# A four-layer graph network on one core: layer 0 in nine blocks instead of eight, its layernorm split over three engines, and the dense part fused in place

## The chip, the cores and the metric

The kernel runs on one core of one Trainium2 chip, in one launch. The time is device time in microseconds, the median of three executions. Each profile is of one further execution. PE is TensorE, DVE is VectorE, ACT is ScalarE, POOL is GpSimd, SP is SyncE; PEld is TensorE's loading of weights. L12 means line 12 of the kernel.

## The reference

x is 4096 x 256 in float32, adj is 4096 x 4096 in int32 with ones at a density of 1/128. Four layers follow each other, each `x = x + layer(relu(layernorm(x)), adj)`:

```python
# layer 0: attention, and a dense part on top of it
Wh = h @ W                                      # 4096 x 256
e = Wh @ a_src + (Wh @ a_dst).T                 # one term per row, one per column
e = where(e > 0, e, 0.2 * e)
attn = softmax(where(adj > 0, e, -9e15), axis=1)
h_attn = attn @ Wh
h_enh = silu(ln(Wh @ fe1)) @ fe2                # biases left out in this listing
B, C, dt = split(Wh @ W_bcdt)
ab = (softmax(dt + A) * B) @ abp
hp, z = split((Wh * ab) @ W_hz)
hs = ((hp * silu(z) + hp * D) @ out_w) * (1 + C @ cp_w)
g = sigmoid(silu(ln(concat(h_attn, hs) @ g1)) @ g2)
out = ln(g * h_attn + (1 - g) * hs + h_enh)
# layer 1: mean over neighbours, then a matrix
# layer 2: attention as in layer 0 with slope 0.01, then elu
# layer 3: softmax(Q K^T masked by adj + identity) @ V
```

## The kernel before

x lives in SBUF as `xs`, 32 row tiles of 128 rows. Work is laid out in blocks of `BT` = `RB` = 4 row tiles. The program is written as Python loops; a scheduler then decides where each instruction stands in the queue of its engine, and every engine works through its queue in order. Tiles come from pools with a fixed number of buffers; a tile that takes over a buffer waits until the last use of the tile before it.

**Layer 0, preparation (`block0`, L416).** For each of eight blocks: three units of adj are fetched and turned (`fresh`, L348), four tiles of x are loaded, layer-normed (`preln`, L124: statistics on DVE, the power -1/2 on POOL, and one activation for each tile on ACT), transposed on PE (`transposed_block`, L138: PSUM is copied half by DVE, half by ACT), and multiplied by W (`project`, L201). W carries two more columns, W a_src and W a_dst, which `weights` (L178) computes with DVE, so the product gives Wh and both attention terms. DVE copies the two terms into `sd` (L208), ACT copies the rest into `v` (L209), which has a last column of ones.

**A unit of adj** is 128 rows x 1024 columns. POOL's queue loads it, turning int32 into bf16. PE transposes its eight 128x128 squares into PSUM (`cT`, one buffer), and ACT's exponential makes of 0 and 1 a very large and a very small number ("codes", L362), into `turned`. SP's queue also writes the codes to DRAM (`codesT`), for the later layers.

**Layer 0, attention (class `Attention`).** A block of four row tiles goes over 32 column tiles, two at a time: 16 pairs. `reach` (L216) runs 19 pairs ahead of it, and finds each row's largest logit: DVE takes a running minimum over codes minus the column's term (L229), ACT and PE turn the result, and small DVE instructions make two row terms, `ab`. These are written to DRAM and read back spread over all partitions (`ab_row`, L251 and L253). `logits` (L258) makes y with DVE (L265) and subtracts the codes with POOL (L269). `run` (L271) then lets ACT take the exponential (L295) and PE multiply y by v (L306), three pairs later, summing in four accumulators, the last column being the softmax denominator. A float32 product is two passes on PE. Between these steps `ahead` (L367) turns one more unit of a later block.

**Layer 0, dense part (`dense`, L561).** Eight blocks, each a long chain of products, layernorms, and gates over four row tiles. It is a generator with some thirty steps; a new block starts every sixteen steps, so that two are in work at a time. After each of the first sixteen steps `count` (L550) counts one unit of adj for layer 1 with two Sign activations on ACT (L556); `ask` (L544) loads the unit ahead of time through POOL's queue, into four buffers. Towards the end of a block, `f` (L682) receives the gate's product; its buffer is also that of `henh` (L645). `f` is then layer-normed, scaled and added to `xt` (x read again) by POOL (L695, L696), which writes `xs`.

**Layer 1 to 3** follow with their own preparations. Layer 2 uses the same class `Attention`.

## Time and profile before

| | us |
|---|---|
| median of three runs | 3072.19 (3071.23 to 3072.98) |
| profiled execution | 3071.94 |
| its span, first to last instruction | 3070.0 |
| first product of layer 0's attention | at 118.9 |
| its last | at 638.4 |
| end of layer 0's dense part | at about 1250 |
| layer 1 | 1250 to 1550 |
| preparation of layer 2 | 1550 to 1618 |
| layer 2's attention | 1618 to 2097 |
| layer 3 | 2097 to 3070 |

In lines that list busy times, the columns are the stretch, its length, then the busy time (and number of instructions) of PE, PEld, DVE, ACT and POOL, the granted clock of TensorE as a share of full speed, the mean busy share of the 16 DMA engines, and the GB/s that they moved. In the timeline a line gives start, duration, engine, line, operation, out<-in, shapes and count; in brackets stands the idle time of the engine before it and what ended it. In lists of waits, "A <- B: 44.3, 7, 7.0" means that A waited for B 44.3 us in total, seven times, at most 7.0 us. "q" after an engine's name is its queue of DMA issues.

### The profile page before, as it was taken

What the parts mean: (1) busy time and instruction counts of PE and PEld (TensorE: products, weight loads), DVE (VectorE), ACT (ScalarE), POOL (GpSimd) and SP (SyncE); (2) the same over time, 40 slices, a digit from 0 to 9 for tenths busy, and PEclk for the clock granted to TensorE, in tenths of its full rate; (3) what the DMA queues carried; (4) which work ended last, traced back from release to release, by engine and by line L of the source; (5) the groups of instructions that cost most, each with busy time, mean ns of one, the idle gap of its engine ahead of it and who ended that gap; (6) DMA issues with size and microseconds to landing.
All of it is one profiled execution on the core that took longest, in us unless ns stands there. A gap on an engine that the chain in (4) does not pass through costs nothing.

```text
span 3070.0 us, 34819 instructions
## 1 busy us (share of the span) xinstructions
PE 2868.8 (93%) x13344; PEld 2341.7 (76%) x13344; DVE 1847.3 (60%) x3298; ACT 1271.1 (41%) x1924; POOL 952.6 (31%) x727
## 2 busy tenths in 40 slices
PE   5799999999999999699968999999999999999999
PEld 4688888866565555588857888788888888888888
DVE  5766766424444444544479888845866666666653
ACT  5555665469999962400044434443211211211211
POOL 3556665534544443100016555561000000000000
PEclk9799999999999999799988999999999999999999
DMA  8566665244544420234222222102111111111100
GB/s 208 130 137 143 127 137 132 66 65 73 79 76 77 75 47 7 88 124 142 91 110 76 89 79 72 71 8 69 59 37 46 49 37 43 52 37 40 53 7 7
DMA packets 105366, 235.18 MB, mean 77 GB/s; under 512 B 10704, under 2 KB 26576, under 8 KB 97008
## 3 DMA queue, kind: packets, MB, share of 16 engines
q0 software_dynamic: 39328, 73.56, 15.6%
q1 hardware_dynamic: 64480, 158.68, 15.0%
q8 instruction: 104, 1.70, 0.2%
q10 hardware_dynamic: 1392, 0.72, 0.1%
q14 instruction: 62, 0.51, 0.1%
HBM read 262.22 MB, written 37.81 MB: 98 GB/s over the span
## 4 chain that ended last, share of the span: by engine, by line
PE 26%; issue 25%; DVE 4%; POOL 2%; DMA 1%; ACT 1%; POOLq 0%; DVEq 0%; ACTq 0%
PE acc L306 11%; PE acc L764 8%; PE s L150 3%; PE mm L150 2%; PE acc L1001 2%; DVE run L229 1%; POOL y L269 1%; DVE y L265 1%; DMA turned<-codesT 1%; POOL out_dram L1014 1%; POOL pl_rs L116 0%; DVE pl_st L121 0%; ACT y L295 0%; ACT h L133 0%; DVE hT L109 0%
## 5 line engine op out<-in xcount | busy, mean ns | idle before, releaser
L306 PE MATMUL acc<-v,y 128*128 128x257 f32 x4096 | 927.7, 385 | 46.1 <-ACT y L295 23.5
L306 PEld LDWEIGHTS acc<-v,y 128*128 128x128 f32 x4096 | 776.3, 192 | 160.5 <-ACT y L295 24.1
L269 POOL TENSOR_TENSOR y<-y,turned 128x1024 f32<-128x1024 f32 x256 | 547.1, 2150 | 313.9 <-DVE y L265 267.1
L295 ACT ACTIVATE y<-y,sdst 128x512 f32<-128x512 f32 x512 | 342.9, 714 | 368.1 <-POOL y L269 367.9
L265 DVE SCALAR_TENSOR_TENSOR y<-ab_row,cdst,b 128x512 f32<-128x512 f32 x512 | 361.7, 742 | 187.9 <-PE acc L306 116.6
L1001 PE MATMUL acc<-v,y 128*128 128x257 f32 x2048 | 454.5, 380 | 0.4 <-DVE rden L1009 0.4
L150 PE MATMUL s<-qT,hT 128*128 128x256 f32 x2048 | 445.2, 380 | 0.7 <-ACT qT L949 0.7
L150 PEld LDWEIGHTS s<-qT,hT 128*128 128x128 f32 x2048 | 389.9, 190 | 53.2 <-ACT qT L949 1.4
L1001 PEld LDWEIGHTS acc<-v,y 128*128 128x128 f32 x2048 | 387.9, 190 | 55.1 <-issue 0.8
L994 ACT ACTIVATE y<-y 128x1024 f32<-128x1024 f32 x128 | 132.2, 1055 | 714.3 <-DVE y L993 710.1
L229 DVE SCALAR_TENSOR_TENSOR run<-turned,sd,run 128x512 f32<-128x512 bf16 x496 | 373.0, 752 | 48.4 <-DMA turned<-codesT 26.8
L1014 POOL DMA_DIRECT2D out_dram<-o x32 | 17.4, 542 | 933.7 <-DVE rden L1009 930.5
L556 ACT ACTIVATE sign<-a,limits 128x1024 bf16<-128x1024 bf16 x256 | 293.9, 1148 | 16.1 <-DMA a<-in_adj_dram 10.4
L764 PE MATMUL acc<-v,eq 128*128 128x512 f32 x1024 | 239.3, 395 | 0.0
L963 DVE SCALAR_TENSOR_TENSOR y<-code,s 128x512 f32<-128x512 bf16 x256 | 175.7, 687 | 100.5 <-PE s L150 100.3
L764 PEld LDWEIGHTS acc<-v,eq 128*128 128x128 f32 x1024 | 192.9, 189 | 44.7 <-DVE eq L760 0.3
L993 DVE TENSOR_TENSOR y<-y,top 128x1024 f32<-128x1024 f32 x128 | 146.2, 1214 | 43.0 <-PE top L987 43.0
L970 DVE TENSOR_TENSOR mx<-mx,y 128x512 f32<-128x512 f32 x224 | 154.9, 691 | 7.4
L362 ACT ACTIVATE turned<-cT,log_wide 128x1024 bf16<-128x1024 bf16 x128 | 141.4, 1105 | 32.1 <-PE cT L357 31.9
L150 PE MATMUL mm<-kept 128*128 128x512 f32 x288 | 135.6, 605 | 9.4 <-ACT kept L508 7.3
L760 DVE TENSOR_SCALAR eq<-code 128x4096 fp32r<-128x4096 bf16 x32 | 73.4, 2292 | 114.9 <-PE acc L764 114.9
L357 PE MATMUL cT<-identb,adj_t 128*128 128x128 bf16 x1024 | 83.2, 226 | 38.1 <-ACT turned L362 19.5
(209 smaller groups left out, 2779.4 us busy)
## 6 DMA issues: line engine op xcount, KB each, us to landing
adj_t<-in_adj_dram POOLq DMA_DIRECT2D x128, 256.0 KB, 4.6
codesT<-turned SPq DMA_DIRECT2D x32, 1024.0 KB, 5.3
a<-in_adj_dram POOLq DMA_DIRECT2D x128, 256.0 KB, 4.2
code<-codesT SPq DMA_DIRECT2D x128, 256.0 KB, 3.8
turned<-codesT SPq DMA_DIRECT2D x32, 1024.0 KB, 4.8
code<-codesT SPq DMA_DIRECT2D x64, 512.0 KB, 4.9
ab_row<-l_ab_d SPq DMA_DIRECT2D x16, 512.0 KB, 4.7
xs<-in_x_dram SPq DMA_DIRECT2D x8, 512.0 KB, 8.3
```

Source lines behind the costliest of these rows:

```text
L150: nc.tensor.matmul(out=ps, lhsT=lhsT_of(k), rhs=rhs_of(k), start=(k == 0), stop=(k == n - 1))
L229: nc.vector.scalar_tensor_tensor(st["run"], code, self.sd[:, j, 1:2], st["run"], ALU.subtract, ALU.min)
L265: nc.vector.scalar_tensor_tensor(y[:, :, k, :], st["ab"][:, 0, :, :], self.cdst[:, c + k : c + k + 1], st["b"], ALU.add, ALU.max,)
L269: nc.gpsimd.tensor_tensor(y, y, mask[:, :, c % QT : c % QT + 2, :], ALU.subtract)
L295: nc.scalar.activation(y[:, :, k, :], y[:, :, k, :], AF.Exp, bias=self.sdst[:, c + k : c + k + 1],)
L306: nc.tensor.matmul(out=accs[b][r], lhsT=y[:, r, k, :], rhs=self.v[:, c + k, :], start=(c + k == 0), stop=(c + k == NT - 1),)
L556: nc.scalar.activation(sign, came[g], AF.Sign, bias=limits[:, v : v + 1], accum_out=over[:, t, v, q : q + 1],)
L764: nc.tensor.matmul(out=acc, lhsT=eq[:, ts(c, P)], rhs=v1[:, c, :, :], start=(c == 0), stop=(c == NT - 1),)
L963: nc.vector.scalar_tensor_tensor(y[:, :, c : c + 2, :], st["code"][:, :, c : c + 2, :], -BIG / UNIT, ps, ALU.mult, ALU.add,)
L970: nc.vector.tensor_tensor(mx, mx, y[:, :, c : c + 2, :], ALU.max)
L993: nc.vector.tensor_tensor(part, part, top, ALU.subtract)
L1001: nc.tensor.matmul(out=accs[r], lhsT=st["y"][:, r, c, :], rhs=v3[:, c, :], start=(c == 0), stop=(c == NT - 1),)
```

## The change

**Two half blocks.** The blocks of layer 0's attention are now nine: rows 0 and 1, rows 2 and 3, then seven of four. A block needs the codes of its own rows and the column terms of all rows, so the first needs 8 units of adj, not 16. The units come in the order of the blocks. The first 8 of them have buffers of their own in the preparation; one unit, not three, is turned for each block of x, and twelve before the attention's loop begins. codesT is written once both halves are there.

**Row terms of the first block.** They are spread over the partitions by PE, as four products with a 4 x 4 x 128 selection matrix `picks`, and copied by ACT and DVE; all other blocks go through DRAM as before.

**Layernorm.** The mean is taken off with a change of sign, by ACT (one tile of four), DVE (two) and POOL (one). The transposed copy in PSUM gets relu with scale -1 on ACT, both halves. The factor 1/sqrt(var) is applied after W, in ACT's copy of the product.

**v.** It has the ones in its first column, Wh in the next 256, and the two attention terms behind. One ACT copy of 258 columns takes the place of DVE's copy of two and ACT's of 256, in layers 0 and 2. `sd` is gone.

**Loads.** W and the a rows go through ACT's queue in layer 0, all eight loads of x are issued at the beginning, from SP and ACT in turn, and four units of adj ahead of all of POOL's other loads. W_bcdt and the rows with it are loaded by SP in the last block of the attention into free adj buffers, and the six small DVE instructions with them move there too. The cast of `identb` is on POOL.

**Dense part.** `f` is written into `xs` itself (the block's attention result, last read before), no longer into `henh`'s buffer. `count` asks for one unit less ahead, with the four buffers left.

```diff
-    nc.vector.tensor_copy(identb, ident)
+    nc.gpsimd.tensor_copy(identb, ident)
...
-            evac(k, hT[:, k, :], ps)
+            if turned:
+                nc.scalar.activation(hT[:, k, :], ps, AF.Relu, scale=-1.0)
+            else:
+                evac(k, hT[:, k, :], ps)
...
-                nc.vector.tensor_copy(sd[:, t, :], ps[:, D : D + 2])
-                nc.scalar.copy(self.v[:, t, 0:D], ps[:, 0:D])
+                row = self.v[:, b * BT + i, 1 : D + 3]
+                if rs is None:
+                    nc.scalar.copy(row, ps)
+                else:
+                    nc.scalar.mul(row, ps, rs[:, i : i + 1])
...
+            if self.picks is not None and b == 0:
+                ps = self.ps_top.tile([P, 2 * n, P], F32, tag="top", name="spread")
+                for k in range(2 * n):
+                    nc.tensor.matmul(
+                        out=ps[:, k, :], lhsT=self.picks[:, k, :], rhs=abT, start=True, stop=True
+                    )
+                for v in range(2):
+                    evac(1 - v, st["ab"][:, v, :, :], ps[:, ts(v, n), :])
+                return
             nc.sync.dma_start(out=self.ab_d[b].rearrange("v r i -> (v r) i"), in_=abT)
...
+            cuts = [(0, 2), (2, 2)] + [(t, RB) for t in range(RB, NT, RB)]
+            units = [
+                (at // RB, q, r % RB)
+                for at, n in cuts for q in range(NQ) for r in range(at, at + n)
+            ]
+            def needed(n):
+                b, c = n // PPB, n % PPB
+                if b >= len(cuts):
+                    return len(units)
+                return cuts[b][0] * NQ + cuts[b][1] * NQ * (c + 1) // PPB
...
             def ahead(n):
-                if n + UPB + FRESH < NRB * UPB:
-                    fresh(n + UPB + FRESH)
+                fresh(needed(n + PPB + FRESH))
...
+                load(4)
+                att.weights(
+                    wp, work, w["L0_gnn_W"], (w["L0_gnn_a_src"], w["L0_gnn_a_dst"]), nc.scalar
+                )
+                for b in range(NB):
+                    (nc.scalar if b % 2 else nc.sync).dma_start(
+                        out=xs[:, ts(b, BT), :],
+                        in_=x[ts(b, BW), :].rearrange("(t p) d -> p t d", p=P),
+                    )
                 def block0(b):
                     xb = xs[:, ts(b, BT), :]
-                    for g in range(3 * b, 3 * b + 3):
-                        fresh(g)
...
-                    preln(small, xb, xb)
+                    for i in range(BT):
+                        mean = mv[:, i, 0:1]
+                        if i == 0:
+                            nc.scalar.activation(
+                                xb[:, i, :], xb[:, i, :], AF.Identity, scale=-1.0, bias=mean
+                            )
+                        else:
+                            (nc.gpsimd if i == BT - 1 else nc.vector).tensor_scalar(
+                                xb[:, i, :], xb[:, i, :], mean, -1.0, ALU.subtract, ALU.mult
+                            )
+                    rs = rstd_of(small, mv, BT, "pl")
+                    load(2 * b + 6)
+                    fresh(b + 1)
                     yield
-                    hT = transposed_block(work, pst, xb, "hT")
+                    hT = transposed_block(work, pst, xb, "hT", turned=True)
                     yield
-                    att.project(b, hT, psm)
+                    att.project(b, hT, psm, rs)
                     yield
-                    for n in range(2 * b, 2 * b + 2 if b < NB - 1 else PPB + LEAD):
+                    for n in range(2 * b, 2 * b + 2):
                         att.reach(n)
                 run_staggered([block0(b) for b in range(NB)], 2)
...
+                fresh(needed(PPB + FRESH - 1))
+                for n in range(PPB, PPB + LEAD):
+                    att.reach(n)
...
             def count(g):
-                ask(g + AHEAD)
+                ask(g + AHEAD - 1)
...
-                f = d.tile([P, BT, D], F32, tag="henh", name="f")
+                f = ha
...
-                nc.gpsimd.tensor_tensor(ha, f, xt, ALU.add)
+                nc.gpsimd.tensor_tensor(f, f, xt, ALU.add)
...
-            ask(AHEAD - 1)
+            ask(AHEAD - 2)
```

## The prediction

> **What bounds the kernel now.** I began with the slices of the page, to see where TensorE is not full, then took busy times by stage.
>
> ```profile
> PE   5799999999999999699968999999999999999999
> ACT  5555665469999962400044434443211211211211
> PEclk9799999999999999799988999999999999999999
> ```
>
> ```profile
> 118.90:184.70 65.80, 64.09 (x349) 55.19 (x350) 49.18 (x82) 40.41 (x57) 49.72 (x32) 0.97 0.39 81
> 184.70:638.40 453.70, 438.44 (x2499) 377.62 (x2497) 281.45 (x457) 240.57 (x332) 271.15 (x190) 1.00 0.51 115
> 638.40:1250.00 611.60, 557.44 (x2049) 354.82 (x2047) 272.32 (x565) 484.28 (x767) 267.21 (x246) 0.97 0.40 63
> 1550.00:1618.30 68.30, 42.15 (x197) 33.13 (x197) 59.51 (x189) 35.09 (x78) 10.98 (x10) 0.82 0.24 100
> ```
>
> Columns: stretch, length, then PE, PEld, DVE, ACT, POOL busy, clock, DMA share, GB/s. The attention of layer 0 (its first block, then the other seven) is full of PE. The dense part is not: PE 557 of 612 us, ACT 484. The preparation of layer 2 leans on DVE (59.5 of 68.3). Layers 1 and 3 are not edited. The 118.9 us ahead of attention are the first thing to look at:
>
> ```profile
> 40.00:60.00 20.00, 17.29 (x132) 14.34 (x131) 12.67 (x35) 18.82 (x35) 6.39 (x10) 1.00 0.81 184
> 60.00:80.00 20.00, 18.33 (x147) 15.81 (x146) 13.01 (x34) 19.89 (x37) 4.91 (x10) 1.00 1.02 230
> 80.00:100.00 20.00, 14.18 (x118) 11.89 (x117) 16.22 (x36) 13.40 (x20) 4.84 (x9) 0.81 1.05 240
> 100.00:120.00 20.00, 4.12 (x27) 3.34 (x27) 10.30 (x16) 5.12 (x6) 6.17 (x6) 0.50 0.75 189
> ```
>
> From 40 to 80 us ACT is the limit (38.7 of 40). Then a chain takes over, which the timeline shows:
>
> ```profile
> 96.98 0.34 SPq L251 DMA_DIRECT2D l_ab_d<-abT_sb  x1
> 104.30 0.34 SPq L253 DMA_DIRECT2D ab_row<-l_ab_d  x1
> 113.73 0.59 ACT L263 COPY b<-ab_row 128x512 f32<-128x512 f32 x1 [8.34 <-DMA ab_row<-l_ab_d]
> 118.91 23.15 PE L306 MATMUL acc<-v,y 128*128 128x257 f32 x96 [12.45 <-ACT y L295]
> ```
>
> The row terms of block 0 go to DRAM and come back spread over the partitions: 16.7 us, with 1 MB writes of codesT in the same queue. In the dense part, the waits:
>
> ```profile
> POOL a L548 <- ACT sign L556: 125.2, 58, 7.4
> DVE henh L649 <- POOL xs L696: 44.3, 7, 7.0
> PE mm L150 <- DVE henh L649: 25.3, 7, 4.2
> ACT sign L556 <- DMA a<-in_adj_dram: 10.4, 8, 3.9
> ```
>
> f and henh share one buffer. So henh of a block waits until f of the block before has left POOL (L696), and PE stops 3.1 to 4.2 us, seven times. After five of the seven stops the next 24 passes take 7.04 to 7.13 us, after two 5.45: the clock fell.
>
> **The change, part by part.** All sums are against the profiled execution (3071.94 us, span 3070.0), which lies inside the three runs (median 3072.19), so a difference carries over.
>
> *1. Preparation of layer 0.* Per block of four tiles ACT now has: one centring (0.60 from L133), two hT copies (0.59 each, L107), four copies of v (0.37 each, L209), one code tile (1.11, L362): 4.4 us, where it had three code tiles, four L133, four copies and one hT: 7.7. DVE loses four copies of sd (0.16) and half of hT, gains two centrings; its min-scan is half as wide. POOL gains one centring, at about 0.8 (half of its 128x512 at 1.56), and once the cast of identb (0.19). The copies of v now carry rs, so POOL's pow (1.03) must be done by then; transposes and hT, some 3 us, cover it. PE keeps 8 transposes (1.04) and 16 passes (3.65), with one code tile (0.61), and waits for both hT copies, with little between them in its new order. So a block is about 1.04 + 1.7 + 3.65 + 0.2 = 6.6 us. The same loop in layer 2 goes at 6.1 us a block without code tiles (the mm rows at 1573.39, 1579.52, 1585.50, 1591.83, 1597.46). I take 6.4.
>
> When does it start? All loads of x are issued at once, four from ACT's queue, behind W and the two a rows, which also left POOL's queue. Two of those issues wait for earlier transfers, and the table load, every centring and copy of ACT stand behind them. DVE's first instruction waits for W and a; all statistics stand behind it. In the profile x arrived block by block between 5.2 and some 33 us, and b_row, issued at 2.36, was there at 13.1. I put DVE's start at 8 us and its step at 2.7 us a block. ACT's new order puts the centrings of blocks 1 to 4 ahead of block 0's last copies, so the first product ends near 24. Seven more blocks at 6.4: 69 us.
>
> *2. From there to the first acc.* The min-scan tail, transposes, m, abT and the row terms took 6.4 us (90.3 to 96.7). The trip through DRAM goes: four products with K = 4 and two copies (about 1.5 us), one copy of b, then DVE, POOL and ACT on a half-size tile, about 3 us where it was 5.2. That is 12 us. PE has six code tiles in its queue among these steps; in this stretch of the profile one took 2.2 us (ACT's 1.11, PE's turn, one PSUM buffer), so 13. First acc near 82 us, not 118.9: **-37**. If x arrives as late as before and a block takes 7: 93. If a block takes 5.6: 74.
>
> Here the Trainium skill speaks against the worth of the edit. DMA: Bandwidth & Descriptors (Anatomy of one DMA) gives about 2.0 us a transfer plus bytes over 436 GB/s. As an estimate, write and read back would be 2.0 + 3.2 = 5.2 us, and layer 2, whose queue is empty there, does show 5.0 (1607.62 to 1612.59). By the rule the edit gains under 4 us; by the row, 15, since here the queue is full of code traffic. I take the row: in the profile the writes stand ahead of it.
>
> *3. Two half blocks.* They replace one block of 65.8 us. Work done before the first acc falls from 32 code tiles to 14, so 28 are turned within the 32 half pairs. PE per half pair: 8 passes 1.74 (half of 3.47) + 0.5 to 0.6 = 2.3. ACT: two exps of 128x256 at about 0.5 (the L133 rows of that size: 1.09 for two, back to back) + 1.11 = 2.1. POOL 1.1 + 0.57 = 1.7. DVE in the second half block: two half logits at 0.4, two full scans at 0.79: 2.4. Engines are so near each other that I take 2.5 a pair: 80 us, **+14**. PE alone would give 73.
>
> Half-size instructions carry their fixed cost twice. VectorE: DVE Perf Modes (TRN2 errata) says that an instruction pays a fixed latency, with a measured fixed term of about 150 cycles. As an estimate, the 0.752 us scan halves to 0.42. By the nearest rows (custom reductions: 128x256 in 418 ns, 128x128 in 285) 256 elements fewer save 0.27, so 0.49. With 128 half instructions for 64 whole, DVE gets 14 us more by the row and 6 by the rule. I take the row; it matters in the second half block only, and is in the 2.5.
>
> *4. Later.* 86 instead of 80 code tiles in the seven whole blocks: 6 x 0.5 = **+3**. The row terms of the second and third blocks still go through DRAM, with less lead (three half pairs, 7.5 us, where it was 12): DVE waits, and behind it stand the scans; PE has about four pairs in hand. **+3**, from 0 to +10. W_bcdt and its rows leave ACT's start-up for SP's queue in the last block: seven issues at 0.32 us, some of them waiting for adj buffers, ahead of the kept loads and behind codesT. PE's 64 us cover them; without that, 2 us. The six small DVE instructions there likewise.
>
> *5. Dense part.* With f in place, henh waits for nothing. The order of PE is unchanged. What takes over? A period with counts and the one without:
>
> ```profile
> 907.70:982.70 75.00, 69.31 (x256) 44.31 (x255) 33.69 (x70) 69.10 (x110) 35.62 (x34) 0.98 0.47 74
> 1132.70:1207.70 75.00, 71.31 (x272) 46.50 (x272) 34.23 (x72) 22.65 (x32) 26.54 (x16) 0.99 0.03 8
> ```
>
> With counts ACT is as full as PE, and it works through Sign tiles in order while PE stops. The copies that PE needs next (whT, comb) stand behind those Signs: at 914.53 ACT waited only 1.0 us for PE, with 0.3 after it. So removing a 3.5 us stop gains about 1.4. Against this, one code tile fewer is asked ahead. In the profile:
>
> ```profile
> 906.35 1.13 POOL L548 DMA_DIRECT2D a<-in_adj_dram  x2
> 912.26 1.15 ACT L556 ACTIVATE sign<-a,limits 128x1024 bf16<-128x1024 bf16 x1 [0.66 <-DMA a<-in_adj_dram]
> ```
>
> The place in POOL's order stays (behind L695, L696), but its load now serves the Sign pair that came one earlier, at 909.1. If it lands at 912 again, ACT waits 2.9 instead of 0.66, and perhaps 0.5 at the next. Net +1.3 a period, five times: +6.5. POOL no longer waits 125 us for Signs; little of that was on PE's path. The last two stops have no Signs beside them: -5.2 (3.5, and 1.7 of clock) and -3.1. Sum **-2**; from -34 (all seven stops, 25.3 + 5 x 1.7, if ACT gives way) to +8.
>
> *6. Layer 2.* The copies of sd go:
>
> ```profile
> L208 DVE COPY sd<-mm 128x2 f32<-128x2 f32 x32 | 5.0, 155 | 3.0 <-PE mm L150 2.2
> ```
>
> 5.0 us of DVE, and ACT's copy no longer waits for them; PE paces part of it: **-3** (0 to -6).
>
> Sum: -37 + 14 + 3 + 3 - 2 - 3 = -22. **3050 us.**
>
> **Rivals.** (a) The stops in the dense part are gained in full, since loads land in time or ACT catches up: 32 us more, 3018. For it: POOL is never held by a Sign. Against: ACT at 69 of 75. (b) The start gains little: x and W come as late as before, acc at 95: 3063. For it: DMA share near 1 throughout; against: 12 code tiles fewer to fetch. (c) Slower: code tiles become the bound of the half blocks. They have one PSUM buffer; a turn took 2.2 us with ACT free, and two exps (1.0) with their gaps (0.3) may stand in it: 3.5 a pair in place of 2.5 over 28 pairs, +28: 3078. It decides from about 3.3 a pair on. For it: ACT's queue is in order and the buffer is single. Against: in whole blocks ACT finds time while PE works 3.5 us; here it has 1.74.
>
> **How the numbers follow.** Forecast 0.45 (own range 3040 to 3061), (a) 0.22, (b) 0.20, (c) 0.13. 0.2% is 6 us, about what a measurement tells from no change, so faster is under 3066: nearly all of the forecast and of (a), two thirds of (b): 0.79. Same: 0.11. Slower: (c) mostly: 0.10. The range runs from (a) with a better start, 3012, to just short of (c), 3075.
>
> **What would show it.** First acc at 74 to 93 us with no ab DMA ahead of it; the two half blocks in 73 to 88; no wait of henh on POOL; Sign's wait on its loads up from 10.4 us; dense part within 10 us of 611.6; layer 2's preparation 3 us shorter. Wrong: a first acc after 100, half pairs over 3.3, or a dense part under 590.

## The result, and the profile after

The changed kernel takes **3059.24 us** (median of five, 3058.36 to 3059.55) where the kernel before took 3072.19 (five runs, 3071.23 to 3072.98). The ratio is 0.9955, with a 95% interval of 0.9942 to 0.9968: 13 us less. The profiled execution took 3058.37 us, its span is 3056.6 (before: 3071.94 and 3070.0).

The slices of the page of after, as before TensorE, ACT and the granted clock:

```profile
PE   6989999999899999799969999999999999999998
ACT  5766555379999963400054434443212111111111
PEclk9999999999999999899979999999999999999999
```

The hole in the second slice of PE (7 before) is closed and the one in front of it is smaller, but the third slice, from 153 to 229 us, has gone from 9 to 8. In the dense part, slices 9 to 16, little has changed: one slice of PE is at 8 where all were at 9. The stretches of after, in the columns of before (length, PE, PEld, DVE, ACT, POOL, clock, DMA share, GB/s): the first half block, the second, what follows until rows 4 to 7 begin, the seven whole blocks, the dense part.

```profile
82.60:122.40 39.80, 37.88 (x227) 31.09 (x228) 31.14 (x70) 28.68 (x50) 27.11 (x31) 0.93 0.85 199
122.40:161.50 39.10, 37.44 (x269) 31.76 (x269) 34.28 (x69) 30.94 (x49) 25.05 (x30) 1.00 0.97 223
161.50:169.20 7.70, 1.87 (x18) 1.36 (x15) 4.54 (x9) 3.86 (x6) 3.43 (x4) 0.82 0.98 256
169.20:623.90 454.70, 439.40 (x2478) 377.85 (x2479) 288.58 (x476) 244.77 (x337) 281.21 (x193) 1.00 0.50 113
623.90:1235.20 611.30, 557.63 (x2049) 354.40 (x2047) 281.09 (x568) 484.20 (x768) 272.39 (x249) 0.96 0.40 63
```

The third line is new: 7.7 us between the half blocks and the first whole block in which PE works for 1.87. By stages, with the same marks in both traces (the dense part ends with POOL's last add, at 1255.66 us before; the 1250 that the prediction used cut its end off):

| stage | before | after | change | predicted |
|---|---|---|---|---|
| up to the first acc | 118.9 | 82.6 | -36.3 | -37 |
| rows 0 to 3 (one block, two half blocks) | 65.8 | 78.9 | +13.1 | +14 |
| until rows 4 to 7 begin | 0 | 7.7 | +7.7 | +3 |
| seven whole blocks | 453.8 | 454.8 | +1.0 | +3 |
| dense part | 617.2 | 611.1 | -6.1 | -2 |
| layer 1, preparation of layer 2 | 362.7 | 360.3 | -2.4 | -3 |
| attention of layer 2 | 477.7 | 480.2 | +2.5 | 0 |
| layer 3 to its last acc | 969.2 | 969.2 | 0 | 0 |
| from there to the end | 4.8 | 11.8 | +7.0 | 0 |
| sum | 3070.0 | 3056.6 | -13.4 | -22 |

Three things need a reason: the 7.7 us stall, the dense part, and 7 us at the very end, where the change edits nothing.

**The start.** Timeline of after, ACT and PE, at the end of the preparation; the row terms now come from products (spread):

```profile
74.50 0.24 ACT L258 COPY abT_sb<-abT 4x128 f32<-4x128 f32 x1
77.17 0.37 ACT L107 COPY ab_row<-spread 128x256 f32<-128x256 f32 x1 [2.43 <-PE spread L264]
78.83 0.38 ACT L281 COPY b<-ab_row 128x256 f32<-128x256 f32 x1
82.60 1.66 PE L325 MATMUL acc<-v,y 128*128 128x257 f32 x3 [0.40 <-ACT y L314]
```

From abT (the two row terms, turned) to the copy of b (the second of them, spread) it takes 4.3 us, with no transfer in it. In windows of 20 us:

```profile
40.00:60.00 20.00, 18.89 (x123) 15.65 (x121) 8.62 (x24) 14.89 (x27) 2.78 (x3) 1.00 0.10 18
100.00:120.00 20.00, 18.81 (x132) 15.45 (x131) 13.52 (x28) 15.26 (x25) 12.42 (x16) 1.00 0.96 210
120.00:140.00 20.00, 18.64 (x132) 15.95 (x131) 20.00 (x41) 17.06 (x28) 15.73 (x19) 1.00 0.98 224
140.00:160.00 20.00, 19.00 (x135) 15.82 (x134) 15.92 (x31) 15.19 (x25) 11.45 (x15) 1.00 0.98 229
```

The work has changed places. From 40 to 60 us PE is the limit now, and the DMA engines stand nearly idle (share 0.10; before 0.81). From 100 to 160 they are full (0.96 to 0.98), since the loads that the old preparation made ahead now fall beside the half blocks. And from 120 to 140 DVE has not a moment free: the second half block scans whole tiles for rows 4 to 7. A half pair takes 39.8/16 = 2.49 us in the first half block and 2.44 in the second; over each of them PE is the fullest engine (37.88 of 39.80 us and 37.44 of 39.10, DVE 31.14 and 34.28).

**The stall before rows 4 to 7.** Timeline of after, ACT, SP and PE:

```profile
152.08 0.25 ACT L258 COPY abT_sb<-abT 8x128 f32<-8x128 f32 x1 [0.41 <-PE abT L256]
152.36 0.28 SPq L270 DMA_DIRECT2D l_ab_d<-abT_sb  x1
153.61 0.32 SPq L427 DMA_DIRECT2D codesT<-turned  x1
154.56 0.32 SPq L271 DMA_DIRECT2D ab_row<-l_ab_d  x1
164.03 0.59 ACT L281 COPY b<-ab_row 128x512 f32<-128x512 f32 x1 [3.54 <-DMA ab_row<-l_ab_d]
166.08 0.78 PE L402 MATMUL cT<-identb,adj_t 128*128 128x128 bf16 x8 [4.50 <-ACT turned L407]
```

The terms of rows 4 to 7 need 11.9 us from abT to the copy of b, and by then the half block that should cover them has run out. ACT stands at the copy, and the code tiles for PE stand behind it.

**The dense part.** Waits of after from 624 to 1235 us (total, times, longest):

```profile
POOL a L639 <- ACT sign L647: 121.8, 55, 7.4
...
PE tp L598 <- ACT whT L599: 16.0, 4, 5.0
...
ACT sign L647 <- DMA a<-in_adj_dram: 12.9, 10, 4.2
...
DVE henh L740 <- PE mm L153: 12.5, 14, 1.3
```

henh waits for nothing but its product. POOL waits for Signs as before (121.8 us; 125.2). In place of seven stops at henh (25.3 us) PE has four at the transposes behind whT (16.0); in the 7 us after three of them the granted clock was 0.70 to 0.76. One of them in the timeline of after, PE and ACT:

```profile
827.74 1.97 PE L598 MATMUL tp<-ident,hs 128*128 128x128 f32 x8 [4.86 <-ACT whT L599]
```

```profile
825.98 1.15 ACT L647 ACTIVATE sign<-a,limits 128x1024 bf16<-128x1024 bf16 x1
827.12 0.56 ACT L599 COPY whT<-tp 128x512 f32<-128x512 f32 x1
```

PE had ended those transposes of whT at 821.4; the copy came after the last of a row of Signs that began at 814.1.

A block ends with POOL's add to xs. The first ends 119 us into the dense part in both kernels. From there, add to add, the seven periods were 74.2, 74.6, 75.3, 74.6, 73.1, 73.1, 53.2 us and are now 76.0, 75.3, 75.3, 75.3, 74.1, 67.6, 48.5. The last two, in which ACT has no Signs left (the last one ends at 1125.6 us before and at 1115.2 now), gained 5.5 and 4.7; the five before them, in which ACT counts throughout, lost 4.2 together. (Counted from henh to henh, the gain seems to lie in the first period, 77.9 to 69.5, and 3.8 us seem lost behind the last henh. But henh itself no longer waits, so that mark has moved against the rest of its block.)

**Layer 2's preparation.** Copies of v, before and after, grouped by line (busy, mean ns, idle before them and its cause):

```profile
L209 ACT COPY v<-mm 128x256 f32<-128x256 f32 x32 | 11.7, 368 | 8.8 <-DVE sd L208 8.7
```

```profile
L214 ACT COPY v<-mm 128x258 f32<-128x258 f32 x32 | 11.6, 369 | 10.4 <-PE mm L153 10.3
```

ACT's copy no longer waits for DVE, it waits for PE, and not shorter (10.4 us; 8.8). DVE, the fullest engine there, has its 5.0 us of copies less. From layer 1's last acc to layer 2's first it takes 2.2 us less here, and 2.1 to 4.2 less in all twelve kernels below.

**The end.** From the last acc to the end of the span it took 4.8 us and takes 11.8, with the same instructions, and the last two stores land 2.0 us after their issue in both. What differs is an instruction that the page does not count, POOL's closing drain at the line of the launch. Before, then after (count, shortest, median and longest in ns, first and last start):

```profile
L1065 POOLq DRAIN  x3: 46/93/2465, 3066.7 to 3069.7; - x3
```

```profile
L1160 POOLq DRAIN  x3: 46/93/9454, 3046.4 to 3056.3; - x3
```

It took 2.5 us and takes 9.5.

### The profile page after: what moved, and what is told of

Its sections match the earlier page's. It is cut to its first block, busy times and chain, and to the rows that moved or that the text cites. A ratio compares the mean times of both kernels' runs of the same rounds, so it can differ in the third digit from the quotient of the medians.

```text
span 3056.6 us, 34943 instructions
## 1 busy us (share of the span) xinstructions
PE 2874.6 (94%) x13353; PEld 2341.0 (77%) x13353; DVE 1854.3 (61%) x3304; ACT 1275.1 (42%) x1944; POOL 965.4 (32%) x749
## 4 chain that ended last, share of the span: by engine, by line
issue 26%; PE 17%; DVE 3%; POOL 2%; DMA 1%; ACT 1%; POOLq 0%; DVEq 0%; ACTq 0%
PE acc L325 11%; PE s L153 3%; PE acc L1096 2%; DVE run L237 1%; PE mm L153 1%; DVE y L283 1%; POOL y L287 1%; DMA turned<-codesT 1%; POOL out_dram L1109 1%; ACT y L314 0%; POOL pl_rs L116 0%; ACT hp L889 0%; PE q_ps L153 0%; ACT h L133 0%; DMA ab_row<-l_ab_d 0%
## 5 line engine op out<-in xcount | busy, mean ns | idle before, releaser
L287 POOL TENSOR_TENSOR y<-y,turned 128x1024 f32<-128x1024 f32 (+1 forms) x272 | 550.1, 2037 | 301.5 <-DVE y L283 261.9
L314 ACT ACTIVATE y<-y,sdst 128x512 f32<-128x512 f32 (+1 forms) x544 | 350.7, 689 | 360.7 <-POOL y L287 360.5
L283 DVE SCALAR_TENSOR_TENSOR y<-ab_row,cdst,b 128x512 f32<-128x512 f32 (+1 forms) x544 | 368.6, 711 | 162.5 <-PE acc L325 103.0
L237 DVE SCALAR_TENSOR_TENSOR run<-turned,v,run 128x512 f32<-128x512 bf16 (+1 forms) x527 | 379.8, 721 | 58.3 <-DMA turned<-codesT 28.0
L153 PE MATMUL mm<-kept,zT 128*128 128x256 f32 x512 | 116.8, 381 | 0.0
```

Source lines behind the costliest of these rows:

```text
L153: nc.tensor.matmul(out=ps, lhsT=lhsT_of(k), rhs=rhs_of(k), start=(k == 0), stop=(k == n - 1))
L237: nc.vector.scalar_tensor_tensor(st["run"], code, dst, st["run"], ALU.subtract, ALU.min)
L283: nc.vector.scalar_tensor_tensor(y[:, :, k, :], st["ab"][:, 0, :, :], self.cdst[:, c + k : c + k + 1], st["b"], ALU.add, ALU.max,)
L287: nc.gpsimd.tensor_tensor(y, y, mask[:, :, c % QT : c % QT + 2, :], ALU.subtract)
L314: nc.scalar.activation(y[:, :, k, :], y[:, :, k, :], AF.Exp, bias=self.sdst[:, c + k : c + k + 1],)
```

## The experiments

In the runs below the kernel before lay between 3065 and 3077 us (medians 3071.3 to 3072.7), a wider spread than in the first comparison, so a few us are read from the stages of the profiled executions, one for each kernel; layer 3, of which only e11 edits anything, its stores, took 969.2 to 969.5 us in all of them. Columns: median, ratio to the kernel before with interval, first acc, start of rows 4 to 7, end of layer 0's attention, length of the dense part, time from the last acc to the end.

| kernel | median | ratio | first acc | rows 4-7 | L0 end | dense | end |
|---|---|---|---|---|---|---|---|
| before | 3072.2 | | 118.9 | 184.7 | 638.5 | 617.2 | 4.8 |
| changed | 3059.2 | 0.9955 (0.9942 to 0.9968) | 82.6 | 169.2 | 624.1 | 611.1 | 11.8 |
| e1_whole | 3051.7 | 0.9939 (0.9922 to 0.9956) | 96.9 | 163.4 | 619.1 | 609.6 | 11.8 |
| e2_own_f | 3068.5 | 0.9987 (0.9981 to 0.9994) | 81.5 | 168.5 | 624.2 | 618.7 | 11.8 |
| e3_old_ask | 3058.9 | 0.9958 (0.9943 to 0.9973) | 82.5 | 168.3 | 627.1 | 611.4 | 11.8 |
| e4_dram | 3069.9 | 0.9990 (0.9981 to 1.0000) | 90.1 | 181.8 | 641.8 | 610.9 | 11.8 |
| e5_spread3 | 3052.0 | 0.9930 (0.9915 to 0.9945) | 80.8 | 160.5 | 621.0 | 611.2 | 11.8 |
| e6_codes_late | 3057.2 | 0.9951 (0.9936 to 0.9966) | 82.1 | 169.9 | 627.9 | 609.9 | 11.8 |
| e7_pool_w | 3050.7 | 0.9925 (0.9910 to 0.9940) | 75.6 | 171.4 | 624.2 | 610.5 | 4.8 |
| e8_dve_copies | 3070.0 | 0.9991 (0.9984 to 0.9998) | 81.9 | 169.3 | 627.8 | 623.6 | 11.8 |
| e9_whole_pool | 3040.4 | 0.9893 (0.9879 to 0.9908) | 94.0 | 159.8 | 616.8 | 609.2 | 4.8 |
| e10_early_pool | 3041.6 | 0.9893 (0.9876 to 0.9909) | 83.1 | 162.7 | 620.5 | 610.3 | 4.8 |
| e11_out_sp | 3052.4 | 0.9928 (0.9913 to 0.9943) | 81.5 | 168.2 | 624.3 | 608.8 | 4.0 |
| e12_pool_rows | 3054.2 | 0.9943 (0.9926 to 0.9959) | 82.0 | 166.3 | 628.0 | 608.6 | 7.2 |

Every edit is against the changed kernel.

**Are the half blocks worth their price?**

```diff
-            cuts = [(0, 2), (2, 2)] + [(t, RB) for t in range(RB, NT, RB)]
+            cuts = [(t, RB) for t in range(0, NT, RB)]
...
-                    load(2 * b + 6)
-                    fresh(b + 1)
+                    load(3 * b + 6)
+                    fresh(3 * b + 3)
```

(`picks` grows to 8 x 8 x P, and the products go in two groups of four.)

> The changed kernel with one whole first block (four row tiles) in place of the two half blocks; its row terms are still spread by products (eight of them, in two groups), and 24 instead of 12 code tiles are turned before the first acc. Changed kernel: first acc at 82.6 us, first acc of rows 4 to 7 at 169.2. Theory (the half blocks give back 20.8 us, of which 7.7 is a stall at their end, and save only some 12 us ahead of the first acc, since twelve code tiles at 1.11 us of ACT are what they save): first acc at 93 to 96, the whole block 66 us, rows 4 to 7 begin at 159 to 162, so 7 to 10 us faster than the changed kernel: 3049 to 3052 us. Rival (the half blocks are worth their price): first acc at 104 or later, rows 4 to 7 begin at 169 or later, 3059 us or more.

First acc at 96.9 us, 14.3 later, and rows 4 to 7 at 163.4, 5.8 earlier; the block of four took 66.5 and nothing stopped after it. As they stand, the half blocks are not worth their price. By the traces 32 code tiles are turned before the first acc here and 14 in the changed kernel, so 18 move across it (the 24 and 12 of the expectation are those before the loop), and every instruction of half size pays its fixed part again (a scan of 128x256 took 0.48 us, one of 128x512 0.75). But 8.1 of the 20.1 us that they give back are PE's stop ahead of rows 4 to 7. Where that is gone, in e5, rows 4 to 7 begin at 160.5 and the attention ends at 621.0, against 163.4 and 619.1 here: the two ways are then about even.

**What holds up rows 4 to 7?** First the way of the terms:

```diff
-            if self.picks is not None and b == 0:
+            if self.picks is not None and b < 3:
```

(and products in two groups for the block of four)

> The changed kernel with the row terms of its first three blocks (both half blocks and rows 4 to 7) spread by products; only from the fourth block on do they go through DRAM. In the changed kernel the terms of rows 4 to 7 took 11.9 us from abT to the copy of b, with a 1 MB write of codes in the same queue, and TensorE ran for 1.9 us out of the 7.7 before 169.2. Theory (the trip makes that stall; by products it takes about 5 us and DVE goes on): the stretch from first acc to the last of rows 0 to 3 shrinks from 86.1 to 79 to 81 us, 3052 to 3054 us. Rival (the terms are simply late, since the scan of rows 4 to 7 ends at 150 us): 84 to 87, 3057 to 3060.

As the theory had it: from the first acc to DVE's last reciprocal for rows 0 to 3 it took 79.7 us (86.1 in the changed kernel), and rows 4 to 7 began at 160.5, 0.7 us after PE's last product for rows 0 to 3, where it had been 8.1. The window from 161 to 170 us, in the changed kernel and in this one:

```profile
161.00:170.00 9.00, 3.15 (x27) 2.51 (x26) 5.84 (x11) 4.66 (x7) 4.23 (x4) 0.80 0.91 228
```

```profile
161.00:170.00 9.00, 8.26 (x50) 6.87 (x49) 9.00 (x15) 6.45 (x10) 6.71 (x5) 1.00 0.85 210
```

So the trip through DRAM makes the stall. Of the 8.7 us that rows 4 to 7 come earlier (the first acc did by 1.8), 3.1 are left at the end of the attention; the next boundary, whose terms still travel, stops PE for 2.5 us at 221 (1.1 in the changed kernel), and smaller gaps take the rest. Then what makes the trip slow:

```diff
-                if c % QT == 0 and (at + size) % RB == 0:
+                if c % QT == 4 and (at + size) % RB == 0:
```

> The changed kernel with each write of codes to DRAM issued two pairs later; the row terms keep their place and their way through DRAM, so no 1 MB write is issued between the write and the read of the terms of rows 4 to 7. Theory (the queue holds the terms up, for 4 of 11.9 us): abT to the copy of b 7 to 9 us, the stretch from first acc to the end of rows 0 to 3 from 86.1 to 81 to 84, 3054 to 3058. Rival (all DMA engines are full, whatever stands in this queue): 11 to 13 us as before, 85 to 88, 3058 to 3061.

By its number the rival: abT to the copy of b took 13.1 us (151.58 to 164.66), and rows 4 to 7 began at 169.9. But the run doesn't test what it was made for. SP's queue of this run still has a write of codes between the write and the read of the terms, where the changed kernel has one:

```profile
151.86 0.28 SPq L270 DMA_DIRECT2D l_ab_d<-abT_sb  x1
153.11 0.32 SPq L427 DMA_DIRECT2D codesT<-turned  x1
154.35 0.32 SPq L271 DMA_DIRECT2D ab_row<-l_ab_d  x1
```

So it leaves open whether that write or the full DMA engines (share 0.94 over this trip in both kernels) make it slow. The changed kernel has one trip to compare with, that of rows 2 and 3: no write of codes lies between its write and its read, and from abT to the copy of b it took 7.0 us (110.65 to 117.68), while the share stood at 0.96. The packets of the read began 1.5 us after its issue there, and 4.0 us after it for rows 4 to 7, behind most packets of the 1 MB write. That speaks for the write having a part in it, but the read for rows 2 and 3 is half as large, and no run takes the write away.

**What is the spreading by products worth in the first block?**

```diff
-            att.picks = picks.tile([4, 4, P], F32, name="picks")
-            nc.vector.tensor_copy(att.picks, ...)
```

> The changed kernel with the row terms of the first half block sent through DRAM, as all others are, in place of the four products. Before the change this trip took 16.7 us in the first block. Theory (the trip was long because writes of codes stood ahead of it in SP's queue; in the changed kernel none does at that moment): issue to landing 5 to 8 us, first acc at 84 to 88 us instead of 82.6, 3060 to 3064 us. Rival, the row used in the prediction (16.7 us against about 4): first acc at 94 to 97, 3070 to 3074.

Between the two. Timeline of this run, SP, then ACT:

```profile
70.62 0.33 SPq L270 DMA_DIRECT2D l_ab_d<-abT_sb  x1
74.14 0.35 SPq L422 DMA_DIRECT2D codesT<-turned  x1
76.04 0.32 SPq L271 DMA_DIRECT2D ab_row<-l_ab_d  x1
```

```profile
86.81 0.38 ACT L281 COPY b<-ab_row 128x256 f32<-128x256 f32 x1 [3.84 <-DMA ab_row<-l_ab_d]
```

The trip took 16.2 us from the issue of the write to the copy of b, as long as before the change (16.7): the theory that no write of codes would be in the way was wrong, two are, at 70.10 and 74.14. That the first acc came only 7.5 us later is because abT was ready 4.2 us earlier in this run (70.34, not 74.50). More came behind it. The terms of rows 2 and 3 took 10.7 us from abT to the copy of b (7.0 in the changed kernel), PE was busy for only 14.88 of the 20 us from 120 to 140, and rows 4 to 7 began 12.6 us later than in the changed kernel; the seven whole blocks took 5.1 us longer. The profiled execution (3074.2) lies above the median of 3069.9.

**The dense part: what is f in place worth, and what the later asking?**

```diff
-                f = ha
+                f = d.tile([P, BT, D], F32, tag="henh", name="f")
...
-                nc.gpsimd.tensor_tensor(f, f, xt, ALU.add)
+                nc.gpsimd.tensor_tensor(ha, f, xt, ALU.add)
```

> The changed kernel with f in the buffer that henh uses, as before the change; all else as changed. Changed kernel: dense part 611.3 us (from the end of layer 0's attention to the last add on POOL), before 617.4. Theory (f in place is what shortened the dense part, and the loads that are asked later take some of it back): the waits of henh on POOL return, the dense part is 617 to 624 us, 3065 to 3072. Rival (the dense part is set by ACT, f in place is worth nothing): 609 to 613, 3058 to 3060.

Dense part 618.7 us, 7.6 more. The five periods with Signs are back at 371.5 us (before: 371.7; changed: 375.9), the last two at 73.1 and 55.0, and the stops are those of before, to the tenth:

```profile
DVE henh L740 <- POOL xs L788: 44.3, 7, 7.0
...
PE mm L153 <- DVE henh L740: 25.3, 7, 4.2
```

```diff
-                ask(g + AHEAD - 1)
+                ask(g + AHEAD)
...
-            ask(AHEAD - 2)
+            ask(AHEAD - 1)
```

> The changed kernel with the code tiles of the counts asked one unit earlier, as before the change; f stays in place. Theory of the prediction (Sign waits about 1.3 us more in each of five periods): Sign's wait on its loads falls below 10 us, the dense part from 611.3 to about 605, 3052 to 3054 us. Rival 1 (the loads were in time, Sign's wait rose by 2.5 us only): dense part 610 to 612, 3057 to 3060. Rival 2 (asking earlier puts POOL behind the Signs again, and its work for PE is late): dense part 613 to 618, 3060 to 3066.

Rival 1: dense part 611.4, every period within 0.3 us of the changed kernel's. Sign's wait on its loads fell by 1.2 us in all, and PE's stops at whT stayed:

```profile
PE tp L598 <- ACT whT L599: 16.0, 4, 5.0
...
ACT sign L647 <- DMA a<-in_adj_dram: 11.7, 10, 3.9
```

So f in place is worth 7.6 us, the later asking costs nothing that can be told, and what the five periods lost is not its doing. That loss isn't a fixed one: all kernels of the table with f in place and the copies as they were have the last two periods at 67.6 and 47.7 to 48.5, and the five at 373.5 to 376.2, 1.8 to 4.5 more than before, with dense parts of 608.6 to 611.4.

**Is it the copies of whT and comb on ACT?**

```diff
-                        onto if k else nc.scalar.copy,
+                        onto,
...
-                        onto if k % 2 else nc.scalar.copy,
+                        onto,
```

> The changed kernel with all six copies of whT and comb in the dense part on DVE, where three of six were on ACT, behind five pairs of Signs. In the changed kernel PE's transposes wait 16 us for them in four stops of 3.1 to 5.0 us, after each of which the clock falls for some passes. Theory (those copies stand between PE and the gain): the stops at whT go, each of five periods from 75.2 to 71 to 73 us, dense part from 611.1 to 590 to 600, 3038 to 3048 us. Rival (ACT is the bound of a period as such, 69 of 75 us; the stop moves on to the next thing that PE wants from ACT): periods 74.5 to 75.5, 607 to 611, 3055 to 3060.

Neither. It is 12.5 us worse: dense part 623.6, the five periods 78.2, 77.9, 76.2, 77.6, 77.7, the last two as they were. The stop at whT is gone, and PE stops at what ACT gives it next, the layernormed t and the transposed dt:

```profile
PE tp L598 <- ACT t L614: 26.5, 21, 4.1
ACT sign L647 <- DMA a<-in_adj_dram: 20.8, 12, 4.8
...
PE mm L153 <- ACT kept L599: 11.1, 7, 2.8
```

ACT was busy for 69.1 us of a period in both kernels, and the period is 77.9 us in one (817.4 to 895.3) and 75.3 in the other. So it is not its busy time alone that sets the period. That it is where its Signs stand against what PE waits for fits the new stops, and is not shown. Why the new order is worse by two microseconds a period, and why the Signs then wait longer for loads, stays open.

**The end, and where W is loaded.**

```diff
-                    wp, work, w["L0_gnn_W"], (w["L0_gnn_a_src"], w["L0_gnn_a_dst"]), nc.scalar
+                    wp, work, w["L0_gnn_W"], (w["L0_gnn_a_src"], w["L0_gnn_a_dst"]), nc.gpsimd
```

> The changed kernel with W and the two a rows of layer 0 loaded through POOL's queue again, as before the change, so that POOL issues 305 transfers as before and not 302. What is looked at is the end: from the last acc to the end of the span it took 4.8 us before and 11.8 in the changed kernel and in all four runs so far, and POOL's closing drain 2.5 and 9.45. Theory (the drain's length follows from what POOL issued in the whole kernel): drain 2.5, end 4.8. Rival (it follows from something else in the change): 9.45 and 11.8. The start may move by -2 to +5 us, apart from that.

The theory: drain 2.457 us, end 4.8. And the first acc came 7.0 us earlier, which neither expected. ACT's queue at the start, changed kernel, then this one:

```profile
2.33 12.79 ACTq L519 DMA_DIRECT2D xs<-in_x_dram  x4
15.15 1.28 ACT L534 ACT_TABLE_LOAD   x1 [15.15 <-issue]
```

```profile
0.73 2.62 ACTq L519 DMA_DIRECT2D xs<-in_x_dram  x4
5.57 1.28 ACT L534 ACT_TABLE_LOAD   x1 [5.57 <-DMA xs<-in_x_dram]
```

With three loads ahead of them, ACT's four issues of x last until 15.1 us, and its first work is behind them; without, they are done at 3.4 and ACT waits only for x. So moving three small loads from POOL to ACT cost 7 us at the first acc and 7 at the end. But of the first nothing is left later on. Rows 4 to 7 begin no earlier (171.4): the copy of b for their terms stands at 164.4 as in the changed kernel, and PE waits the longer, 6.5 us up to 166.

```diff
-                nc.gpsimd.dma_start(out=out[ts(t, P), :], in_=o)
+                nc.sync.dma_start(out=out[ts(t, P), :], in_=o)
```

> The changed kernel with the output rows stored through SP's queue, not POOL's; POOL issues 270 transfers, the last of them long before the end. Theory (POOL's closing drain of 9.45 us is what stands between the last store and the end): POOL reaches its drain early, the end takes 3 to 5 us in place of 11.8, 3050 to 3053 us. Rival (something else ends there, and the drain only waits with it): 11 to 12 us as before, 3058 to 3060.

The theory. The end takes 4.0 us. POOL's drain (270 transfers) is still 8.3 us long, but it begins at 2091 us, beside layer 3:

```profile
L1160 POOLq DRAIN  x3: 46/93/8322, 2091.3 to 3046.0; - x3
```

```diff
-                        nc.sync.dma_start(out=part, in_=src.partition_broadcast(P))
+                        eng = nc.gpsimd if name in ("fe1_b", "g1_b", "out_b") else nc.sync
+                        eng.dma_start(out=part, in_=src.partition_broadcast(P))
```

> The changed kernel with three small loads of the last block of layer 0's attention (the rows fe1_b, g1_b and out_b) issued by POOL instead of SP. POOL then issues 305 transfers, as before the change, but W and the a rows stay in ACT's queue. So far POOL's closing drain took 2.46 us in the three kernels with 305 transfers, and 9.45 in those with 302. Theory (the length of the drain follows from the count of POOL's transfers, not from which they are): drain 2.5, end 4.8, start as in the changed kernel (first acc 81 to 83), 3050 to 3054 us. Rival (it follows from the packets or their sizes, or from the loads of W at the start): drain 8 to 9.5, end 11 to 12, 3057 to 3061.

Half of it came true. With 305 transfers, three of them others than before, the drain is short again, and the first acc is where it was (82.0):

```profile
L1161 POOLq DRAIN  x3: 46/102/2462, 3048.9 to 3051.8; - x3
```

But the end took 7.2 us, not 4.8: POOL issued the last two stores from 3048.36 on, 2.2 us after DVE was done, where the changed kernel issues the first of them 0.3 us before DVE is done; the trace shows nothing that it waited for. So the short drain goes with the count, in five kernels of five, and not with W being among the loads; but POOL can lose time just ahead of the drain instead.

**Two versions that put it together.**

e9_whole_pool is e1 and e7 in one.

> The changed kernel with one whole first block and with W and the a rows back in POOL's queue. By the runs before, the first takes the start of rows 4 to 7 from 169.2 to 163.4 us, and the second the first acc 7.0 us forward (ACT no longer stands behind its issues of x until 15.2 us) and the end from 11.8 to 4.8. Theory (the two add up, since the whole block leaves the DMA engines room): first acc at 89 to 92, rows 4 to 7 begin at 155 to 158, end 4.8, 3034 to 3038 us. Rival (as with the half blocks, what the start gains is lost again to full DMA engines by rows 4 to 7): rows 4 to 7 at 162 or later, 3041 to 3045.

3040.4 us. The end is 4.8; the first acc came 2.9 us earlier than in e1, not 7, and rows 4 to 7 began at 159.8, between the two theories. With three code tiles a block PE and ACT are both nearly full from 40 to 60, and the DMA engines as well. Between 20 us and the first acc PE's main wait is for ACT's turning of code tiles (10.5 us in 14 waits), so ACT holds this preparation up again, as before the change; what the full DMA engines add is not separated:

```profile
40.00:60.00 20.00, 19.03 (x149) 15.88 (x148) 9.62 (x19) 18.03 (x29) 6.90 (x11) 1.00 1.01 226
```

e10_early_pool keeps the half blocks, takes the stall away by products and fetches and turns more ahead:

```diff
-    FIRST = 8
+    FIRST = 12
...
-                    load(2 * b + 6)
-                    fresh(b + 1)
+                    load(min(3 * b + 6, 20))
+                    fresh(2 * b + 1)
```

(with the edits of e5 and e7)

> The changed kernel, half blocks and all, with W and the a rows in POOL's queue, the row terms of the first three blocks spread by products, 20 instead of 16 code tiles fetched while the preparation runs (from 40 to 60 us its DMA engines stood at 0.10), and 15 instead of 8 of them turned there. Theory (what the half blocks lose is lost to DMA engines that are full from 100 to 160 us, because the loads come late): first acc at 77 to 82, rows 4 to 7 begin at 154 to 158, end 4.8, 3032 to 3038 us. Rival (the half blocks are bound by their own instructions, 2.47 us a pair, whenever the codes come): rows 4 to 7 at 159 to 163, 3038 to 3043.

By its number the rival. Rows 4 to 7 began at 162.7, 79.6 us after the first acc, still 2.49 us a pair, although the DMA share fell (0.40 from 80 to 100 us, 0.67 to 120). But that mean hides two changes. From its first acc to the next block's, the first half block took 35.4 us (40.9 in the changed kernel), with PE full; from there to its last product the second took 41.9 (37.6), with DVE full from 120 to 140 again:

```profile
100.00:120.00 20.00, 20.00 (x134) 16.63 (x133) 14.68 (x32) 13.84 (x25) 11.37 (x14) 1.00 0.67 131
120.00:140.00 20.00, 18.84 (x130) 15.75 (x130) 20.00 (x40) 15.29 (x26) 13.46 (x16) 1.00 0.99 213
```

So earlier codes do make the first half block faster, and the second gives it back. What the two cost together is set by their own instructions rather than by the loads; which engine sets it in the second isn't shown (from 119.5 to 160.4 us PE was busy for 38.85 of 40.90, DVE for 34.36). With 3041.6 us this kernel stands beside e9 within what the runs can tell; both are over 17 us faster than the changed kernel.

## Why the prediction was right, and where not

3050 us were forecast, with an own range of 3040 to 3061; it became 3059.2, faster by 13 and not by 22. The direction and the range held; the 9 us between the two numbers are in the terms below.

**Right, with its mechanism.** The start (-37; -36.3), though its parts were off both ways: the first block's products were done at 30.7 us instead of 24 (they began at 24.1, and their sixteen passes took 6.58 us where the next blocks took 3.81), then 5.5 us a block instead of 6.4, and 13.5 from the last product (69.1) to the first acc for 13. That these cancel to within a microsecond is luck. That ACT's issues of x would stand ahead of its work was said, but not that W in front of them is what makes them stand: e7 puts 7.0 us on that. The half blocks (+14; +13.1; 2.5 us a pair; 2.44 to 2.49). The trip through DRAM: weighed between 16.7 by the row and 5.2 by the Trainium skill, DMA: Bandwidth & Descriptors (Anatomy of one DMA); e4 measured 16.2. (The page gives its figure for transfers that GpSimd issues; these are SP's. In layer 2, where no writes of codes are in the way, it came out all the same: 5.0.) Half-size scans: 0.49 by the row and 0.42 by VectorE: DVE Perf Modes (TRN2 errata); the 128x256 scans took 0.48 to 0.49. (The estimate of 0.42 is 256 elements and 150 cycles; the same count gives 0.69 for the whole scan, which took 0.75.) The layer 2 copies (-3; -2.4, though not by ACT's wait). Code tiles in the whole blocks (+3; +1.0). In the dense part, the last two blocks, which have no Signs beside them (-8.3; -10.2).

**Wrong in size: the row terms of the second and third blocks.** +3, with up to +10 allowed; 7.7. The step saw the shorter lead (7.5 us where it was 12) and let the pairs that PE has in hand cover most of it; but the trip took 11.9 us, with a write of codes between its write and its read, and with DMA engines that are full (0.94). By products, in e5, the stop is gone. That the loads which leave the preparation would fall beside the half blocks and fill the DMA engines there (0.96 to 0.98 from 100 to 160) is a consequence of its own first step that the prediction did not draw; how much of the 11.9 us it makes stays open.

**Wrong in two terms of three: the dense part.** "Sum -2" hid +13.5 for later loads (2.7 us of wait in each of five periods) and -7 for the five stops beside Signs, next to the -8.3 for the last two. The first is 0 by e3. That ACT takes over in those five periods was right, even to the copies of whT; that this still gains 1.4 a period was not, they lose 0.8. The sum of the three came out at -6.1, near -2, because the first two errors have opposite signs. Nor did POOL's wait for Signs go (121.8 us).

**Missing: the end.** The prediction counted what W's move did to ACT's queue and not what it did to POOL's. +7.0 us, shown by e7 and e11, though what ties the length of the drain to the loads is open. With this one term it would have said 3057.

**Missing: layer 2's attention, +2.5.** In the other kernels with the same code for it the stage takes 477.0 to 480.6 us (before: 477.7), so most of it varies from one execution to the next.

**The rivals.** (a), all stops gained, fell: beside Signs nothing was gained. (b), the start gains little, fell: 82.6. (c), one PSUM buffer of code tiles binds the half blocks, fell at 2.5 us a pair; whether PE or DVE, which the prediction had at 2.3 and 2.4, sets the pace there is not shown.

## What to carry to other kernels

Work that is taken out of a start-up phase doesn't vanish: ask which transfers and instructions it takes along, and whether the stretch they land in has DMA engines and a lead to spare; here half-size blocks brought the first product 14 us forward and gave back 20, 8 of them in one stop. When transfers are moved between queues, count what stands behind them on the new queue and what the old one does without them, up to its closing drain; keep the last stores of a kernel away from a queue that has a long drain. Removing a wait in a part where another engine is nearly as full moves the stop and gains only where that engine is idle; price the periods one by one, not their mean.

## What the runs showed of the hardware that was not expected

POOL's closing drain took 2.46 us in the kernel before and in the four others whose POOL issues 305 transfers, 9.45 in the changed kernel and the seven others with 302, and 8.32 in the one with 270. It stands between the last store and the end when POOL issues that store, and costs nothing when it doesn't (4.0 us in e11). POOL has waits that nothing shown ends. Two of them, at the loads for the counts, are in both kernels (20.9 us before, 19.5 after). Two others are in the kernel before alone:

```profile
POOL adj_t L354 <- issue: 7.3, 1, 7.3
POOL out_dram L1014 <- issue: 2.5, 1, 2.5
```

e7, e9 and e10 have both, at the same places, ahead of POOL's 113th and 303rd transfer; the changed kernel and those with 302 transfers have neither, and a drain that is 7.0 us longer; e12 has one of 2.5 us alone, ahead of its last two stores. So the 7 us may be a piece of POOL's own work that falls beside other work or into the drain by how its transfers are counted out. No run here settles that, and e12, with the short drain and no wait of 7 us, doesn't fit it well.

Four issues of x on ACT's queue took 2.6 us with nothing ahead of them and 12.8 us behind three loads.
